# Four-layer graph network: reloads of a split matrix in small transfers, a ring of four row buffers, and one row block of layer 3 cast inside layer 2

## The chip, the cores and the metric

The kernel runs on one core of a Trainium2 chip. A core has TensorE (PE; its weight loads are listed as PEld), VectorE (DVE), ScalarE (ACT), GpSimd (POOL), SyncE (SP) and DMA queues. SP, ScalarE and GpSimd issue the transfers. The metric is the device time in microseconds (us); lower is better.

## The reference

Four layers are applied to `x` (4096 rows of 256) with one dense 0/1 adjacency `adj` (4096 x 4096). Each layer ends in `x = layernorm(x + layer(x))`. Layers 0 and 1 (an attention over the graph and a convolution) are not touched. Layers 2 and 3 are, cut to what matters:

```python
# layer 2: two steps; R is adj + identity, each row divided by its sum
for n in range(2):
    A = top_p_attention(Xa)        # softmax of q @ k.T, cut to the largest terms
                                   # that hold 0.9 of a row, renormalized
    Xf = R @ Xf                    # "diffusion"
    Xa = A @ Xa                    # "attention"
    Z = Z + Xf @ U1[n].T + Xa @ U2[n].T
x = layernorm(x + layernorm(x + Z) * ln_g + ln_b)

# layer 3
agg = adj @ x / max(deg, 1)
x = layernorm(x + relu(concat([x, agg]) @ W + b))
```

## The kernel before

**Tiles.** The 4096 rows are 32 row blocks of 128 (`NB = 32`, `P = 128`). `X` holds the attention's right-hand side for all blocks. `XD` holds the right-hand side of the products with the adjacency, 32 blocks of 128 x 512 (a 256-wide value split into two parts of reduced precision); a block is 256 KB. The adjacency lies in DRAM twice: as fp32 (`adjs`) and as bytes (`nad`). An `adj_piece` is the part of one row block that belongs to four column blocks (256 KB); there are three buffers for it. `es[0]`, `es[1]` and `es[2]` each hold one row block of attention scores (128 x 4096, fp32). `kT` holds the keys.

**Step 0 and step 1 of layer 2.** Each step begins with `keys`, `spreads` and the scores of row blocks 0 and 1. Then a loop of `project(step, b)` multiplies two row blocks by two weight matrices into a PSUM tile of two banks (`ps_logit`, two of them). In step 1 SP loads what is already summed for the pair into `xb` (line 1490), ScalarE copies one half of the product to `X` (line 1491) and the other half to a tile called `part` or `dif` in turn (line 1493), GpSimd adds it to `xb` (line 1494) and issues the store back to `xd` (line 1495). There are two buffers of `xb` and one each of `part` and `dif`.

Then a hand-ordered loop (`tc.manual_schedule`) goes over the row blocks. For each block `b` it has eight stages `s`. In a stage TensorE transposes four column blocks of the scores (`turn`, line 1350), ScalarE copies them (line 1352), TensorE multiplies them with `X` (`gather`, line 1359), and beside it TensorE works on diffusion products (`adj_product`, line 180) two or three row blocks ahead. VectorE finds the cut of the next row block meanwhile (`nucleus`, among others lines 1147, 1151, 1201). `scores` (line 993) and its exponentials (line 995) run two row blocks ahead.

**The reloads.** Towards the end of a step no diffusion product is left that reads the old `XD`, and `XD` is loaded with the next right-hand side (`reload`, line 1211, on SP), four blocks at a time: seven reloads of 1 MB at the places in the tuple `freed`, as (row block counted from the last diffusion's, stage). The time that becomes free beside the last row blocks goes to products of the next stage (`early`, with `times`, line 1554): in step 0 the first three row blocks of step 1's diffusion, in step 1 the first five row blocks of layer 3. `early` asks for each piece two pieces ahead (`piece`, line 1545, on SP). SP issues its transfers in order.

**The end of step 1.** Behind the last row block's scores stands a flag (line 1751) that says whether an exact method has to be run (`mend`, line 1217); with these inputs it is not. After it comes a second hand-ordered stretch:

- `load_bytes` fetches the byte adjacency of layer 3's first eight row blocks into `es[2]` and `es[0]` (`nas`, line 1844), 4 MB in all with two transfers issued earlier.
- The attention of row block 31 is gathered in eight steps `g`. `ahead3` multiplies finished rows by layer 3's weight and stores the result to `xtd` and `xo`, for row blocks 29 and 30.
- `closing(31)` runs the two layernorms of the last block on GpSimd and VectorE.
- `cast3` turns the bytes of layer 3's row block 5 into fp32r in `kT`, as four quarters `a[0]` to `a[3]` (line 1856).
- Then nine pieces of `early` are left, a reload of `XD` blocks 28 to 30 (768 KB), two small loads `lasts` into `q`, `product(0)` to `product(3)` with the quarters of block 5 (line 1805), five more pieces of group 7, the rows of block 31 (`turned`, `weighted`, `ahead3` into `XD[31]`), six last matmuls (line 1836), and the load of the next 4 MB of bytes into `X` (`rows`).

**Layer 3.** `ready(b)` casts the bytes of a row block into eight-block pieces, by VectorE (line 1854) and ScalarE (line 1856) in turn; `products(b)` does its 32 matmuls (line 1887); `close(b)` adds bias and weights, applies relu and layernorm and stores. Row blocks 0 to 5 come finished from layer 2. The loop starts so:

```python
            ready(6)
            ready(7)
            rest = [2, 5, 0, 1, 3, 4]
            for b in range(6, NB):
                ps = products(b)
                if b + 2 < NB:
                    ready(b + 2)
```

Of the kernel before, what the change touches and what calls it, by code (L numbers as in the profile page):

```python
# [9 lines left out]
F32 = mybir.dt.float32  # L10
I32 = mybir.dt.int32
F32R = mybir.dt.float32r
# [11 lines left out]
P = 128  # L24
# [31 lines left out]
class Net:  # L56
# [757 lines left out]
    def layer2(self):  # L814
        nc, tc, NB, D, X, N = self.nc, self.tc, self.NB, self.D, self.X, self.N
        A = 64
        HALF = N // 2
        with ExitStack() as ctx:
# [388 lines left out]
            def reload(src, a, b):  # L1207

                for k in range(a, b, 4):
                    to = min(k + 4, b)  # L1210
                    nc.sync.dma_start(XD[:, k:to].bitcast(F32), src[k:to].rearrange("b p s d -> p b s d"))
# [236 lines left out]
            def weighted(xT, pz):  # L1448


                for c in range(2):
                    nc.tensor.matmul(pz, xT[:, c, :], wt[:, c].rearrange("p k m -> p (k m)"),  # L1452
                                     start=(c == 0), stop=(c == 1))
                return pz

            def bank():
                return psum.tile([P, 512], F32, name="ps_tp")

            def project(step, b):


                two = slice(b, b + 2)
                rows = lambda t: t.rearrange("b p d -> p b d")
                pl = psum.tile([P, 2, 512], F32, name="ps_logit", bufs=2)
                if step == 0 and b < 16:
                    pt = bank()
                    for q in range(2):
                        for c in range(2):
                            nc.tensor.transpose(pt[:, (2 * q + c) * P:(2 * q + c + 1) * P],
                                                X[:, b + q, c * P:(c + 1) * P], self.ident)  # L1470
                    xT = work.tile([P, 512], F32, name="aT", bufs=2)
                    nc.scalar.copy(xT, pt)
                    xT = xT.rearrange("p (q c m) -> p q c m", q=2, c=2)
                else:
                    xT = held(step, b, 2)
                for q in range(2):
                    for c in range(2):
                        nc.tensor.matmul(pl[:, q, :], xT[:, q, c, :], wt[:, c].rearrange("p k m -> p (k m)"),
                                         start=(c == 0), stop=(c == 1))
                xb = work.tile([P, 2, D], F32, name="xb", bufs=2)  # L1480
                if step == 0:
                    nc.scalar.copy(XD[:, two, 0, :], pl[:, :, :D])
                    nc.scalar.copy(xb, pl[:, :, D:])
                    nc.vector.tensor_sub(XD[:, two, 1, :], pl[:, :, :D], XD[:, two, 0, :].bitcast(F32))
                    nc.scalar.dma_start(rows(pd[two]), xb)
                    xs = work.tile([P, 2, D], F32, name="part", bufs=1)
                    nc.gpsimd.tensor_add(xs, X[:, two, :], affine.unsqueeze(1).to_broadcast([P, 2, D]))
                    nc.gpsimd.dma_start(rows(xd[two, :, 1, :]), xs)
                else:
                    nc.sync.dma_start(xb, rows(xd[two, :, 0, :]))  # L1490
                    nc.scalar.copy(X[:, two, :], pl[:, :, :D])
                    xs = work.tile([P, 2, D], F32, name=("part", "dif")[b // 2 % 2], bufs=1)
                    nc.scalar.copy(xs, pl[:, :, D:])
                    nc.gpsimd.tensor_add(xb, xb, xs)
                    nc.gpsimd.dma_start(rows(xd[two, :, 0, :]), xb)
# [82 lines left out]
            for step in range(2):  # L1578
# [33 lines left out]
                if step == 0:  # L1612
                    xb = base(step, 0)
# [5 lines left out]
                if step == 0:  # L1619
# [3 lines left out]
                dd = 2 + step  # L1623
                rows_of = (xfd, xtd)[step]
                banks, made = {}, []
                freed = ((-1, 4), (-1, 5), (-1, 6), (-1, 7), (0, 0), (0, 2), (0, 4)) if step == 0 else \
                    ((0, 4), (-1, 5), (-1, 6), (-1, 7), (0, 0), (0, 2), (1, 1))
                freed = {at: g for g, at in enumerate(freed)}
                if step == 0:
                    todo = [(k, g) for g in range(7) for k in range(3)]  # L1630
                else:
# [5 lines left out]
                with tc.manual_schedule(engines=five):  # L1637
                    for b in range(NB - 1):
# [14 lines left out]
                        for s in range(8):  # L1653
# [28 lines left out]
                            for _ in range(pieces[s]):  # L1682
                                next(beside)
                            if (b + dd - NB, s) in freed:
                                g = freed[b + dd - NB, s]
                                reload(rows_of, 4 * g, 4 * g + 4)
                            gather(pa, aTs.pop(0), s)
                            if s == 3 and step == 1 and b - 2 in done:
                                put = ahead3(b - 2, done.pop(b - 2), pz, queue=nc.gpsimd)
# [87 lines left out]
                with tc.manual_schedule(engines=five):  # L1777
# [8 lines left out]
                    for g in range(8):  # L1786
                        if g < 7:
                            aTs.append(turn(es[b % 3], g + 1))
                        if g in (0, 6):
                            put = ahead3(b - 2 + g // 6, h, weighted(xT, bank()))  # L1790
                        gather(pa, aTs.pop(0), g)
                        if g in (0, 3):
                            next(close)
                        if g in (1, 7):
                            whole(put)
                        if g == 5:
                            h = whole(close)
                            xT = turned(h[:, 0], bank())
# [9 lines left out]
                    next(close)  # L1808
                    next(close)
                    self.cast3(nas, 5, a, nc.scalar)  # L1810
                    for _ in range(4):
                        next(beside)
                    next(close)
                    whole(beside)
                    reload(xtd, NB - 4, NB - 1)
                    lasts = []
                    for k in range(2):
                        two = work.tile([P, 2, P], F32R, name="q", bufs=2)
                        nc.sync.dma_start(two.bitcast(F32), self.adjs[2 * k:2 * k + 2, :, NB - 1, :].rearrange("b p i -> p b i"))
                        lasts += [two[:, 0], two[:, 1]]  # L1820
                    rows = [X[:, 8 * i:8 * i + 8, :].rearrange("p b d -> p (b d)").bitcast(U8)
                            .rearrange("p (k i) -> p k i", k=8) for i in range(4)]
                    product(0)
                    for k in range(5):
                        t = piece(1, k, 7)
                        times(banks[k], t, 7, ks=range(3))
                    lasts.append(t[:, 3])
                    h = whole(close)
                    product(1)
                    xT = turned(h[:, 0], bank())  # L1830
                    product(2)
                    pz = weighted(xT, bank())
                    product(3)
                    whole(ahead3(b, h, pz, True))
                    for t, to in zip(lasts + [a[3][:, 7]], [banks[k] for k in range(5)] + [ps]):
                        nc.tensor.matmul(to, t, XD[:, b].rearrange("p s d -> p (s d)"), start=False, stop=True)
                    self.load_bytes(rows, 1, 0)
                self.ahead3 = nas, rows
                self.early3 = [banks[k] for k in range(5)] + [ps]

    def load_bytes(self, nas, it, g):
# [17 lines left out]
    def layer3(self):  # L1859
        nc, tc, NB, D = self.nc, self.tc, self.NB, self.D  # L1860
        G = 8
        with self.ctx3 as ctx:
# [6 lines left out]
            out = self.rows(self.out)  # L1869
            psum, ps1 = self.psum2, self.ps2  # L1870
            nas = self.ahead3
            pieces = {}

            def ready(b):
                it = b * P // self.IT
# [26 lines left out]
                self.layernorm(work, y, h)  # L1902
                nc.scalar.dma_start(out[:, b, :], y[:, 0])

            ready(6)
            ready(7)
            rest = [2, 5, 0, 1, 3, 4]
            for b in range(6, NB):
# [61 lines left out]
```

## Time and profile before

| | |
|---|---|
| time, three runs | 4001.58, 4007.29, 4010.75 us; median 4007.29 |
| the profiled execution | 4011.93 us, span 4010.2 us, mean granted TensorE clock 0.991 |
| busy over the span | TensorE 97%, VectorE 75%, ScalarE 68%, GpSimd 28% |
| step 0 of layer 2, last row block and what follows | about 2604 to 2662 us |
| step 1, projections after the scores | about 2737 to 2797 us |
| step 1, from the flag to layer 3 | about 3735 to 3807 us |
| layer 3 | 3807 us to the end |

A span is the time from the first to the last instruction of the profiled execution. Lines such as L1554 are lines of the kernel before. A wait is put down to the work that ended last ahead of it. Busy times of TensorE come from a model of the pipelined matmul: one of 512 columns is listed with 394 ns, but 32 in a row take 7.47 us, 233 ns each.

### The profile page before, as it was taken

To read this page: it belongs to the slowest core of one execution; us is meant where nothing else is said; L and a number is where in the kernel's file an instruction comes from. 1 tells how busy PE (TensorE), PEld (TensorE's weight loads), DVE (VectorE), ACT (ScalarE), POOL (GpSimd) and SP (SyncE) were. 2 spreads that over 40 slices of the span, in tenths; PEclk is the share of its full clock that TensorE was granted. 3 is DMA by queue.
4 is the path that set the end of the run, shared out by engine and by line. 5 is a ranking of instruction groups with operands and counts; after the bars stand their busy time and mean duration, and the time that the engine had idled before them with its cause. 6 is when DMAs were issued, how large, how long until landed. Compare 5 with 4: busy or idle time off the path is not lost. (4 is left out here: it accounts for less than half of the span.)

```text
span 4010.2 us, 68765 instructions
## 1 busy us (share of the span) xinstructions
PE 3906.8 (97%) x25081; PEld 3377.3 (84%) x25081; DVE 2990.2 (75%) x6647; ACT 2742.6 (68%) x5119; POOL 1136.7 (28%) x1394
## 2 busy tenths in 40 slices
PE   8899998999999899999999999999999999999899
PEld 7899998999999788678888888865888888888687
DVE  7742228999999444567878788837999999999365
ACT  5532228999999322468888888825888888888132
POOL 1321111111344022411111111114555555555211
PEclk9999999999999999999999999999999999999999
DMA  4765557335222498533333333463333333335541
GB/s 130 228 204 176 176 168 224 90 108 136 69 78 70 170 359 324 154 119 96 100 97 101 95 102 92 137 203 105 108 107 104 108 118 99 107 120 184 186 158 49
DMA packets 317403, 557.36 MB, mean 139 GB/s; under 512 B 72646, under 2 KB 139734, under 8 KB 312950
## 3 DMA queue, kind: packets, MB, share of 16 engines
q1 hardware_dynamic: 242368, 396.99, 31.4%
q0 software_dynamic: 32224, 98.75, 7.5%
q10 hardware_dynamic: 42454, 57.04, 4.3%
q8 instruction: 203, 3.33, 0.3%
q14 instruction: 154, 1.26, 0.1%
HBM read 386.71 MB, written 165.94 MB: 138 GB/s over the span
## 5 line engine op out<-in xcount | busy, mean ns | idle before, releaser
L1359 PE MATMUL ps_a<-X,aT 128*128 128x256 f32 x4096 | 970.4, 379 | 1.3 <-ACT h L1500 1.1
L1359 PEld LDWEIGHTS ps_a<-X,aT 128*128 128x128 f32 x4096 | 774.1, 190 | 127.2 <-issue 3.3
L328 PE MATMUL acc<-gm,gt 128*128 128x198 bf16 x8192 | 702.5, 248 | 14.2 <-DVEq L366 5.6
L328 PEld LDWEIGHTS <-gt 128*128 128x128 fp8e4 x8192 | 700.4, 97 | 16.2 <-issue 11.3
L273 ACT ACTIVATE sg<-lpb,nlc 128x1024 fp8e4<-128x1024 f32 x632 | 664.0, 1135 | 48.5 <-DVE gt L275 33.8
L550 PE MATMUL pz<-src,ar 128*128 128x264 f32 x4096 | 513.5, 288 | 20.6 <-DVE ar L540 18.6
L550 PEld LDWEIGHTS pz<-src,ar 128*128 128x128 f32 x4096 | 510.3, 191 | 23.7 <-DVE ar L540 21.3
L180 PE MATMUL ps_r<-XD,adj_piece 128*128 128x512 f32 x1888 | 528.4, 414 | 1.0 <-DMA adj_piece<-adjs 1.0
L1086 ACT ACTIVATE ja<-e,nc 128x2048 uint8<-128x2048 f32 x240 | 480.9, 2004 | 2.0
L1352 ACT COPY aT<-ps_tp 128x512 f32<-128x512 f32 x512 | 296.4, 579 | 216.7 <-PE ps_tp L1350 214.5
L180 PEld LDWEIGHTS ps_r<-XD,adj_piece 128*128 128x128 f32 x1888 | 332.9, 189 | 70.2 <-issue 12.9
L1151 DVE MAX8 cand<-v 128x8 f32<-128x256 f32 x1024 | 347.1, 411 | 4.4
L1201 DVE SCALAR_TENSOR_TENSOR e<-e,edge 128x512 f32<-128x512 f32 x512 | 347.9, 751 | 2.1
L543 ACT ACTIVATE nb<-ar 128x512 uint8<-128x512 f32 x256 | 147.5, 623 | 268.4 <-DVE ar L540 265.2
L1350 PE MATMUL ps_tp<-ident,e 128*128 128x128 f32 x2048 | 307.7, 273 | 0.0
L1147 DVE SCALAR_TENSOR_TENSOR v<-e,hi 128x2048 f32<-128x2048 f32 x128 | 299.8, 2342 | 2.4
L1350 PEld LDWEIGHTS ps_tp<-ident,e 128*128 128x128 f32 x2048 | 256.5, 141 | 51.4 <-issue 0.5
L267 DVE TENSOR_SCALAR sg<-lpb,nlc 128x1024 fp8e4<-128x1024 f32 x384 | 285.2, 778 | 6.6 <-SPq L366 4.4
L995 ACT ACTIVATE e<-ps_logit 128x1024 f32<-128x1024 f32 x256 | 260.2, 1027 | 26.6 <-PE ps_logit L993 26.4
L993 PE MATMUL ps_logit<-kT,q 128*128 128x512 f32 x1024 | 274.1, 409 | 4.0 <-ACT e L995 1.7
L540 DVE CAST ar<-a 128x1024 fp32r<-128x1024 f32 x128 | 88.9, 695 | 248.1 <-PE pz L550 242.4
L802 PE MATMUL ps_adj<-XD,adj_piece 128*128 128x512 f32 x1024 | 244.9, 398 | 1.2 <-POOL ln_var L88 1.2
(396 smaller groups left out, 5577.5 us busy)
## 6 DMA issues: line engine op xcount, KB each, us to landing
adj_piece<-adjs SPq DMA_DIRECT2D x552, 256.0 KB, 2.9
a<-in_adjt_dram SPq DMA_DIRECT2D x256, 256.0 KB, 3.0
adjs<-adj_piece SPq DMA_DIRECT2D x96, 512.0 KB, 3.4
na<-nad SPq DMA_DIRECT2D x64, 512.0 KB, 4.5
lpb<-lpd POOLq DMA_DIRECT2D x32, 512.0 KB, 4.2
nad<-nb POOLq DMA_DIRECT2D x128, 128.0 KB, 2.8
na<-nad ACTq DMA_DIRECT2D x16, 1024.0 KB, 5.6
gmd<-gb POOLq DMA_DIRECT2D x64, 198.0 KB, 3.9
```

Source lines behind the costliest of these rows:

```text
L180: nc.tensor.matmul(ps, a[:, k, :], rhs(jc).rearrange("p s d -> p (s d)"), start=(jc == 0), stop=(jc == self.NB - 1))
L267: nc.vector.tensor_scalar(sg[:, k, :], lpb, nlc[:, 4 * g + k, h:h + 1], 2.0 ** -5, op0=ALU.is_ge, op1=ALU.mult, saturate=False)
L273: nc.scalar.activation(sg[:, k, :], lpb, AF.Sign, scale=-1.0, bias=nlc[:, 4 * g + k, h:h + 1], saturate=False)
L328: nc.tensor.matmul(acc[:, q, :6 * C1], gt[:, k, q * P:(q + 1) * P], gm0[:, jc, :] if head0 else gm[:, jc, hh, :], start=(jc == 0 and q % 2 ...
L550: nc.tensor.matmul(pz[q][:, t, :W], ar[:, q, k, :], src[:, jc, t, s], start=(jc == 0 and s == 0), stop=(jc == NB - 1 and s == 1))
L1086: nc.scalar.activation(ja, e[:, s * HALF:(s + 1) * HALF], f, bias=nc1, accum_out=fs[:, i + s:i + s + 1])
L1147: nc.vector.scalar_tensor_tensor(v, ec, hi, ec, op0=ALU.is_lt, op1=ALU.mult, accum_out=sb[:, s:s + 1])
L1151: nc.vector.max(cand[:, 8 * j:8 * j + 8], v[:, k * 256:(k + 1) * 256])
L1201: nc.vector.scalar_tensor_tensor(ec, ec, edge[:, j:j + 1], ec, op0=ALU.is_ge, op1=ALU.mult)
L1350: nc.tensor.transpose(pt[:, k * P:(k + 1) * P], e[:, jc * P:(jc + 1) * P], self.ident)
L1352: nc.scalar.copy(aT, pt)
L1359: nc.tensor.matmul(pa[:, :D], aT[:, k * P:(k + 1) * P], X[:, jc, :], start=(jc == 0), stop=(jc == NB - 1))
```

## The change

1. **Reloads in small transfers.** `freed` now gives each place a range of blocks. In step 0 the 28 blocks come in ten reloads of 4, 3, 3, 4, 4, 3, 2, 2, 2 and 1 blocks instead of seven of 4; in step 1 in twelve of 3, 3, 3, 3, 2, 2, 2, 2, 2, 2, 2 and 2. Blocks 28 to 30 at the end of step 1 come one at a time: two within the last gather and one after it.
2. **A ring of four in step 1.** Of the sixteen projections of step 1, numbers 2 to 12 take `xb` and the second half's copy from `es[2]`: four places of 512 columns for each. The others keep the tiles they had.
3. **The end of step 1.** Three pieces of `early` move into the last gather (at `g` 3, 5 and 7), as do the two `lasts` loads (at `g` 3); three instead of four pieces stand ahead of the last `next(close)`.
4. **Row block 6 of layer 3 is cast in layer 2.** After `product(i)` has used the quarter `a[i]` of block 5, ScalarE casts the same quarter of block 6 over it; the last one follows the six last matmuls. Layer 3 takes these as `pieces[6]` and its `ready(6)` goes.

```diff
@@ project @@
-                xb = work.tile([P, 2, D], F32, name="xb", bufs=2)
+                nth = (b - 16) % NB // 2
+                ring = [es[2][:, i + nth % 4 * 512:i + nth % 4 * 512 + 512].rearrange("p (q d) -> p q d", d=D)
+                        for i in (0, 2048)] if step and 2 <= nth <= 12 else ()
+                xb = ring[0] if ring else work.tile([P, 2, D], F32, name="xb", bufs=2)
...
-                    xs = work.tile([P, 2, D], F32, name=("part", "dif")[b // 2 % 2], bufs=1)
+                    xs = ring[1] if ring else work.tile([P, 2, D], F32, name=("part", "dif")[b // 2 % 2], bufs=1)
@@ ahead of the loop over row blocks @@
-                freed = ((-1, 4), (-1, 5), (-1, 6), (-1, 7), (0, 0), (0, 2), (0, 4)) if step == 0 else \
-                    ((0, 4), (-1, 5), (-1, 6), (-1, 7), (0, 0), (0, 2), (1, 1))
-                freed = {at: g for g, at in enumerate(freed)}
+                if step == 0:
+                    freed = {(-1, 4): (0, 4), (-1, 5): (4, 7), (-1, 6): (7, 10), (-1, 7): (10, 14), (0, 0): (14, 18),
+                             (0, 1): (18, 21), (0, 2): (21, 23), (0, 3): (23, 25), (0, 4): (25, 27), (0, 5): (27, 28)}
+                else:
+                    freed = {(-1, 5): (4, 7), (-1, 6): (7, 10), (-1, 7): (10, 13), (0, 0): (13, 16), (0, 1): (16, 18),
+                             (0, 2): (18, 20), (0, 3): (20, 22), (0, 4): (22, 24), (0, 5): (0, 2), (0, 6): (2, 4),
+                             (1, 1): (24, 26), (1, 2): (26, 28)}
...
-                                g = freed[b + dd - NB, s]
-                                reload(rows_of, 4 * g, 4 * g + 4)
+                                reload(rows_of, *freed[b + dd - NB, s])
@@ the last gather @@
+                        if g in (3, 5, 7):
+                            next(beside)
                         gather(pa, aTs.pop(0), g)
+                        if g in (2, 4):
+                            k = NB - 5 + g // 2
+                            reload(xtd, k, k + 1)
+                        if g == 3:
+                            lasts = []
+                            for k in range(2):
+                                two = work.tile([P, 2, P], F32R, name="q", bufs=2)
+                                nc.sync.dma_start(two.bitcast(F32),
+                                                  self.adjs[2 * k:2 * k + 2, :, NB - 1, :].rearrange("b p i -> p b i"))
+                                lasts += [two[:, 0], two[:, 1]]
@@ after it @@
                     self.cast3(nas, 5, a, nc.scalar)
-                    for _ in range(4):
+                    for _ in range(3):
                         next(beside)
                     next(close)
+                    reload(xtd, NB - 2, NB - 1)
                     whole(beside)
-                    reload(xtd, NB - 4, NB - 1)
-                    lasts = []
-                    ...
                     product(0)
                     ...
                     lasts.append(t[:, 3])
+                    self.cast3(nas[:1], 6, a[:1], nc.scalar)
                     h = whole(close)
                     product(1)
                     xT = turned(h[:, 0], bank())
+                    self.cast3(nas[1:2], 6, a[1:2], nc.scalar)
                     product(2)
                     pz = weighted(xT, bank())
                     product(3)
+                    self.cast3(nas[2:3], 6, a[2:3], nc.scalar)
                     whole(ahead3(b, h, pz, True))
                     for t, to in zip(lasts + [a[3][:, 7]], [banks[k] for k in range(5)] + [ps]):
                         nc.tensor.matmul(to, t, XD[:, b].rearrange("p s d -> p (s d)"), start=False, stop=True)
+                    self.cast3(nas[3:], 6, a[3:], nc.scalar)
                     self.load_bytes(rows, 1, 0)
-                self.ahead3 = nas, rows
+                self.ahead3, self.sixth = (nas, rows), a
@@ layer3 @@
-            pieces = {}
+            pieces = {6: self.sixth}
...
-            ready(6)
             ready(7)
```

More of the change, by code (lines that the diff above doesn't have):

```diff
@@ L1810, in layer2 @@
                     self.cast3(nas, 5, a, nc.scalar)
-                    for _ in range(4):
+                    for _ in range(3):
                         next(beside)
                     next(close)
+                    reload(xtd, NB - 2, NB - 1)
                     whole(beside)
-                    reload(xtd, NB - 4, NB - 1)
-                    lasts = []
[L1817 to L1820, printed above, removed]
                     rows = [X[:, 8 * i:8 * i + 8, :].rearrange("p b d -> p (b d)").bitcast(U8)
```

## The prediction

> **What bounds the kernel now.** I read the page from the top, then TensorE's waits and timeline in the three stretches where its busy line dips inside layer 2.
>
> ```profile
> PE 3906.8 (97%) x25081; PEld 3377.3 (84%) x25081; DVE 2990.2 (75%) x6647; ACT 2742.6 (68%) x5119; POOL 1136.7 (28%) x1394
> PE   8899998999999899999999999999999999999899
> ```
>
> TensorE is busy for 97% of the span, so an edit pays only where TensorE stands idle or runs at a lower clock: about 103 us in all. The change adds no matmul and takes none away. TensorE's waits at the end of step 0 (2604 to 2662 us), at the start of step 1 (2735 to 2797) and at the end of step 1 (3735 to 3812), as us in total, times, longest:
>
> ```profile
> PE ps_logit L1554 <- DMA adj_piece<-adjs: 6.8, 4, 2.5
> ...
> PE ps_logit L1478 <- ACT part L1493: 1.6, 2, 1.0
> PE ps_logit L993 <- ACT dif L1493: 1.1, 1, 1.1
> PE ps_logit L993 <- ACT part L1493: 1.1, 1, 1.1
> ...
> PE ps_logit L1554 <- DMA adj_piece<-adjs: 6.4, 8, 2.0
> PE ps_tp L1443 <- PEq L1217: 3.8, 1, 3.8
> PE ps_tp L1887 <- DVE adj_piece L1854: 3.3, 1, 3.3
> PE ps_logit L1554 <- POOLq L1217: 1.9, 1, 1.9
> ```
>
> Adjacency pieces come late at both ends, the copies into `part`/`dif` come late at the start of step 1, and layer 3's first cast comes late at the handover. The 3.8 is the branch after the flag and the 1.9 a POOL operation; the change touches neither. Why the pieces are late is in SP's own waits, step 1's start first, then its end:
>
> ```profile
> SPq L1490 <- DMA xd<-xb: 60.3, 14, 10.6
> ...
> SPq L1545 <- DMA xo<-h: 5.3, 1, 5.3
> ```
>
> The first: an `xb` load waits until the store from the same buffer has landed. The second: one piece load of the last stretch stands behind the store of the last row block. What the gaps cost is more than their idle time, as the stretches 3772:3784, 3784:3796 and 3804:3812 show (busy us by engine, granted clock, DMA share, GB/s):
>
> ```profile
> 3772.00:3784.00 12.00, 9.65 (x37) 6.33 (x36) 1.22 (x4) 3.94 (x5) 6.30 (x9) 1.00 0.65 197
> 3784.00:3796.00 12.00, 8.06 (x26) 5.61 (x25) 0.00 (x0) 0.00 (x0) 0.00 (x0) 0.86 0.66 224
> 3804.00:3812.00 8.00, 4.72 (x15) 3.80 (x16) 3.62 (x6) 3.89 (x4) 0.00 (x0) 0.79 0.48 159
> ```
>
> **What the Trainium skill says.** "TensorE: Matmul & The Clock Gate", Part 1, says that TensorE falls to half clock after an idle window and needs some us of work to come back. The trace agrees: clock 0.86 and 0.79 above, and gathers (L1359) of 631 ns after the gap at 2633 where the usual one takes 379. "DMA: Bandwidth & Descriptors", Bandwidth, advises batches of 1 MiB or more. Here a piece of 256 KB lands in 2.9 to 3.1 us and reloads of 1 MB in 7.7 to 8.0 (one measured in each step), but the question is who stands behind the big one. The same page, "Issuing engines are not separate DMA queues", says that all queues share the 16 engines; 414 GB/s at share 1.00 between 3796 and 3804 is this core's ceiling in the trace. "SBUF — State Buffer" says VectorE and GpSimd lock a shared port against each other; POOL's adds (L1494) of 1.25 to 4.35 us for one shape fit that, though part of the long ones is waiting for `xb`.
>
> **1. Handover to layer 3: -4.8.** Now the last matmul of layer 2 starts at 3803.54, VectorE's first cast waits until 3806.49 for the landing of `xo<-h` (4.73 us), and the products start at 3807.28: 3.3 idle. Their first 64 matmuls take 16.45 us, later ones 14.93: 1.5 more at low clock. After: block 6 is cast on ScalarE into `kT` as soon as each quarter of block 5 is used, four times 1.04 us (L1856). Queued behind them on ScalarE are the `xT` copy and the copies for `XD[31]`. The first cast falls under the fifteen `times` matmuls, the second under product(2) (1.86 us), the third under the projection and product(3); the fourth waits for the last matmul, and the 24 products before its quarter last 5.6. So they cost nothing; if that cover failed, 1 to 2 us. Block 7's casts still wait for `xo<-h`, under 7.5 us of block 6. Bounds 2 to 5.
>
> **2. The tail of step 1: -6.8.** From 3771.30 to 3795.13 TensorE does 59 matmuls (nine pieces, product(0), fifteen for group 7). At 7.47 us per 32 they need 13.8; they take 23.8, so 10.0 is lost. The new order puts three pieces (2.8 us) into the gather loop, where their loads are already in; the gather ends at 3774.1 and 47 matmuls remain (11.0). SP's queue, walked with 3.1 us a landing and three buffers: the fourth late piece comes 1.0 late, the sixth 0.7 (block 30's reload, 256 KB instead of 768 KB for three blocks, is ahead of it), the fourth of group 7 1.5. Lost 3.2. In the built queue no piece waits for the last block's store: that wait belongs to the reuse of a DMA semaphore, and the new numbering gives it to an older transfer. The closing chain of the last block (9.0 us from gather end to `h`) starts 2.8 later and is ready at 3783, used about 3790. The reload of block 29 holds SP until its store lands (about 3759); the piece behind it is used at 3774. Bounds 3 to 9.
>
> **3. Step 1's ring: -5.0.** One buffer now goes through load 3.0, add 1.3 to 1.7, semaphore and issue 1.0, store 2.7: 8.2 us, or 4.1 per pair with two buffers; a pair's matmuls need 3.45 (8 at 0.431, from 40 in 17.43). Fourteen pairs at that pace end at 2786.4, then eight transposes and eight score matmuls (2.8) bring the first gather to 2789.2 instead of 2794.68: 5.4. With four places the memory cycle is 2.1 per pair, POOL's add and issue 2.3, ScalarE's two copies 1.2: TensorE sets the pace. VectorE must have row block 0 ready: it waits 6.4 us for POOL's `inv` (L1182), which stands behind the adds; its inputs are there at 2778.5, so the first edges are done about 2781. POOL then waits up to 3 us for VectorE at `above`, which four places bridge. The ring lies in `es[2]`; its last store lands about 2783, before the scores of block 2 overwrite it at 2788. I take 5.0 for a first wait that stays. Bounds 2 to 5.4.
>
> **4. Step 0's reloads: -4.2.** Of four long gaps in pieces two follow 1 MB reloads in the last row block (1.71 and 2.19, 0.2 of small ones); after the second the matmuls run slow for 1.6. Together 5.7. A third of 2.46 follows the 1 MB reload of blocks 28 to 31, which stays. Half-size reloads take 1.3 us less at 390 GB/s (slices of this stretch), about the slack of a piece; I leave 0.5 in each of three stages. Bounds 0 to 5.7.
>
> **5. Step 1's reloads before the flag: -0.3.** One gap of 1.0 behind a 1 MB reload at 3669 may halve; blocks 26 and 27 now come one stage later, 3.6 to 4.5 us before use. Bounds -1 to +1.5. The ten additional transfers in both steps cost SP 0.4 us each to issue; its queue is mostly waiting there. VectorE and ScalarE lose four casts in layer 3, where they wait for TensorE: nothing.
>
> **Sum:** 4.8 + 6.8 + 5.0 + 4.2 + 0.3 = 21.1. The profiled execution took 4011.9 (span 4010.2, 1.7 around it), so it would take 3990.8; it lies 4.6 above the median of 4007.3, so the forecast is **3986**. A difference of 0.2%, 8 us, is about what this measurement can tell from none.
>
> **The rivals.**
> - *Forecast*, 0.56: all five within their bounds, 3980 to 3993.
> - *Bytes, not order*, 0.20: the ends are held by the volume, so steps 2, 4 and 5 give only 1 together and handover and ring 8.8: 3997.5. For it: 263 GB/s between 2604 and 2636 already. Against it: the slices there reach 390, and stage 4 of that block runs three pieces without a wait.
> - *No gap left*, 0.13: 10.0 + 4.8 + 5.4 + 5.7 + 1.0 = 26.9: 3980, down to 3976. Against it: the piece loads still have three buffers and 3 us of latency.
> - *A wait at every small reload*, 0.05, the slower side: SP issues in order, and a reload that waits for an older store or for its semaphore holds the pieces behind it. About fourteen stages now have one; at 2.2 us each (today's gap) this is 31, less 8.8: 4029. It decides from 0.6 us per stage, where gain is used up, and the result is slower beyond 1.2. Against it: in the built queue the waits it adds are on transfers several loads back.
> - *Not what it says*, 0.06: the built order or a bank keeps the handover or the ring as it was, 3991 to 4000.
>
> The range 3977 to 3999 leaves out the slower rival, part of the second and little of the third. Faster 0.86, within 0.2% 0.09, slower 0.05.
>
> **What would show it.** Right: layer 3's products follow the last layer 2 matmul within 0.5 us, their first 64 take about 15; no wait on `part`/`dif` in step 1's projections and the first gather 5 us earlier; SP without the 5.3 on `xo<-h`; the 1.7 and 2.2 gaps under 1. Wrong: piece waits of 1 us in most stages, an idle TensorE behind ScalarE's casts, or a clock under 0.9 after 3772.

## The result, and the profile after

The kernel after takes **3988.26 us** (median of five, 3981.79 to 3996.39) against 4007.29 of the kernel before (five, 4001.58 to 4012.31). The ratio is 0.9953, 95% interval 0.9941 to 0.9965. The profiled execution of after took 3996.39 us, span 3994.6, granted clock 0.991: 8.1 above its own median, where that of before lay 4.6 above.

The page: busy us by engine, then TensorE's busy tenths over 40 slices.

```profile
PE 3901.5 (98%) x25081; PEld 3375.7 (85%) x25081; DVE 2997.9 (75%) x6645; ACT 2747.6 (69%) x5121; POOL 1160.1 (29%) x1394
PE   8899998999999899999999999999999999999899
```

TensorE has the same 25081 matmuls, and the line of tenths is unchanged: the whole result lies under its resolution, in gaps of 0.5 to 5 us. They show in TensorE's waits at the end of step 0 (2604 to 2662 us), the start of step 1 (2735 to 2797) and its end (3735 to 3812):

```profile
PE ps_logit L1557 <- DMA adj_piece<-adjs: 4.2, 3, 2.6
...
PE ps_tp L1350 <- DVE e L1201: 1.9, 2, 1.4
...
PE ps_logit L1557 <- DMA adj_piece<-adjs: 4.5, 5, 1.5
PE ps_tp L1443 <- PEq L1217: 3.8, 1, 3.8
```

Pieces late: 6.8 became 4.2 in step 0 and 6.4 became 4.5 in step 1. The copies into `part` and `dif` hold TensorE no more, but a wait for VectorE's edges has come. No wait for a layer 3 cast is left; the branch after the flag is as it was. (Lines of the kernel after: L1493 is the load of `xb`, L1496 the copy of the second half, L1497 GpSimd's add, L1548 `piece`, L1557 `times`, L1823 `product`, L1852 the last matmuls, L1861 `load_bytes`, L1904 layer 3's products.) SP's own waits, first the start of step 1, then its end:

```profile
SPq L1493 <- DMA xd<-e: 31.2, 7, 10.6
...
SPq L1548 <- PE ps_logit L1557: 19.2, 9, 6.6
SPq L1861 <- DVE adj_piece L1871: 14.9, 1, 14.9
SPq L1211 <- DMA xtd<-part: 7.4, 1, 7.4
```

The loads of the ring still make SP wait, but TensorE waits for nothing behind them. The 5.3 on `xo<-h` is gone; most of what the pieces wait for is a buffer that TensorE frees, as it was before (33.4 there).

The tail in TensorE's timeline (start, us, line, operation, and in brackets the idle time ahead of it), from the last gather to `product(1)`:

```profile
3766.91 3.16 PE L1557 MATMUL ps_logit<-XD,adj_piece 128*128 128x512 f32 x12
3770.91 1.20 PE L1557 MATMUL ps_logit<-XD,adj_piece 128*128 128x512 f32 x4 [0.84 <-DMA adj_piece<-adjs]
3772.85 2.41 PE L1557 MATMUL ps_logit<-XD,adj_piece 128*128 128x512 f32 x8 [0.74 <-DMA adj_piece<-adjs]
...
3780.75 0.96 PE L1557 MATMUL ps_logit<-XD,adj_piece 128*128 128x512 f32 x3 [1.48 <-DMA adj_piece<-adjs]
3782.32 1.46 PE L1557 MATMUL ps_logit<-XD,adj_piece 128*128 128x512 f32 x3 [0.61 <-DMA adj_piece<-adjs]
3783.58 3.12 PE L1823 MATMUL ps_a<-XD,kT 128*128 128x512 f32 x8
3786.54 0.38 PE L1443 MATMUL ps_tp<-ident,h 128*128 128x128 f32 x2
```

And the handover:

```profile
3792.86 0.39 PE L1852 MATMUL ps_logit<-XD,adj_piece 128*128 128x512 f32 x1
3793.09 0.39 PE L1852 MATMUL ps_a<-XD,kT 128*128 128x512 f32 x1
3793.32 7.43 PE L1904 MATMUL ps_tp<-XD,kT 128*128 128x512 f32 x32
3800.59 7.63 PE L1904 MATMUL ps_tp<-XD,adj_piece 128*128 128x512 f32 x32
```

Layer 3 follows without a gap and at full pace: `kT`, cast in layer 2, feeds its first 32 matmuls.

To place the gain I cut each profile at points of TensorE's timeline: **A** from the first gather of step 0's last row block to step 1's main run of projections, **B** from there to the first gather of step 1, **C** on to the first gather behind step 1's flag, **D** on to the matmuls with the last rows, **E** on to layer 3's third row block, **F** the rest.

| | start | A | B | C | D | E | F | span |
|---|---|---|---|---|---|---|---|---|
| before | 2608.25 | 129.67 | 56.76 | 958.13 | 49.57 | 21.20 | 186.62 | 4010.2 |
| after | 2609.45 | 125.31 | 53.69 | 957.19 | 46.30 | 16.12 | 186.54 | 3994.6 |
| after, second profile | 2609.44 | 125.74 | 53.68 | 957.93 | 46.10 | 16.12 | 186.59 | 3995.6 |

Gains 4.4, 3.1, 0.9, 3.3, 5.1 and 0.1, less 1.2 lost ahead of the change: 15.6. The untouched first part took 2600.1 to 2609.5 us in the profiles of this study, so spans are no measure for a part; the stretches are. They vary too, but with one exception, C, the two profiles that have the old form of a part lie outside all that have the new one (kernels whose own edit bears on the stretch left out): A 129.7 and 131.7 against 123.2 to 125.7, B 56.8 and 56.5 against 53.6 to 55.2, D 49.6 and 49.0 against 44.1 to 47.7, E 21.2 and 21.3 against 16.1.

### The profile page after: what moved, and what is told of

Its sections match the earlier page's. It is cut to its first block, busy times and chain, and to the rows that moved or that the text cites. A ratio compares the mean times of both kernels' runs of the same rounds, so it can differ in the third digit from the quotient of the medians.

```text
span 3994.6 us, 68784 instructions
## 1 busy us (share of the span) xinstructions
PE 3901.5 (98%) x25081; PEld 3375.7 (85%) x25081; DVE 2997.9 (75%) x6645; ACT 2747.6 (69%) x5121; POOL 1160.1 (29%) x1394
## 5 line engine op out<-in xcount | busy, mean ns | idle before, releaser
L1350 PEld LDWEIGHTS ps_tp<-ident,e 128*128 128x128 f32 x2048 | 256.8, 142 | 53.6 <-DVE e L1201 3.0
```

What stands on the lines that cost most here:

```text
L1350: nc.tensor.transpose(pt[:, k * P:(k + 1) * P], e[:, jc * P:(jc + 1) * P], self.ident)
```

## The experiments

Each kernel is the kernel after with one edit, where nothing else is said. Times are medians; the kernel before, timed beside each, had medians of 4005.0 to 4007.6. The number behind a median is its ratio to that, with its 95% interval.

### Each part undone

**No ring**: every projection uses `xb`, `part` and `dif` again.

```diff
-                        for i in (0, 2048)] if step and 2 <= nth <= 12 else ()
+                        for i in (0, 2048)] if False else ()
```

> The changed kernel without the ring of four: step 1's projections load, scale and add through the two-deep xb tile and the single part and dif tiles again. Theory (the ring's gain is bounded by VectorE's first edges): the stretch from the first projection of the last 13 pairs to step 1's first gather, 53.7 us in the changed kernel, goes back to 56.8, TensorE's waits there are again on ScalarE's and GpSimd's copies, and the median rises by 2.5 to 3.5 us. Rival (the ring itself cost something, through GpSimd's adds that now run against VectorE's small operations): VectorE's first edge comes no earlier with the ring than without, and the median rises by under 1.5 us. If the prediction's own figure held, it would rise by 5.

B 56.46 instead of 53.69; median 3993.76 (ratio 0.9957, 0.9940 to 0.9974). TensorE's waits in this stretch:

```profile
PE ps_logit L993 <- ACT dif L1496: 1.8, 1, 1.8
PE ps_logit L1478 <- ACT part L1496: 1.6, 2, 1.0
```

The old waits are back and the wait for edges is gone: 2.8 us, the theory's size and about half of the 5 predicted. One bound has been exchanged for another, and a part of the rival is there too: VectorE starts its first edge 48.5 us after the projections' start with the ring and without it. In three of eight profiles with the ring the clock drops after the wait for edges and B is 55.2; there the ring gives 1.3. The timings don't decide the size: the median is 5.5 above that of after, the ratio 0.0004, or 1.6 us, with an interval of 7 us on either side.

**No sixth block**: the four casts out of layer 2, `ready(6)` back in layer 3.

```diff
-                    self.cast3(nas[:1], 6, a[:1], nc.scalar)    # and the three others
-            pieces = {6: self.sixth}
+            pieces = {}
+            ready(6)
             ready(7)
```

> The changed kernel with layer 3's seventh block cast in layer 3 again, after layer 2's last product. Theory: TensorE waits some 3.3 us for the first casts and then runs its first matmuls at a lower clock, so the stretch from the product with the last rows to the third layer 3 block's first product grows by 4.5 to 5.5 us, and the median rises by about 5. Rival (the casts' loads or VectorE's share of them set the time anyway, or the casts in the tail had slowed the tail on ScalarE): under 2.5 us.

E 21.32 instead of 16.12, +5.2; D 46.42, unchanged; median 3996.97 (0.9965, 0.9951 to 0.9979). TensorE's timeline:

```profile
3788.50 0.40 PE L1849 MATMUL ps_a<-XD,kT 128*128 128x512 f32 x1
3792.12 16.71 PE L1900 MATMUL ps_tp<-XD,adj_piece 128*128 128x512 f32 x64 [3.22 <-DVE adj_piece L1867]
```

3.2 us idle and 64 matmuls in 16.7 us. The ratio is 0.0012 above that of after, 4.8 us. The rival falls: D is the same with and without the casts, so on ScalarE in the tail they cost nothing that shows.

**Old reloads**: groups of four blocks at the old places in both steps.

```diff
+                freed = ((-1, 4), (-1, 5), (-1, 6), (-1, 7), (0, 0), (0, 2), (0, 4)) if step == 0 else \
+                    ((0, 4), (-1, 5), (-1, 6), (-1, 7), (0, 0), (0, 2), (1, 1))
+                freed = {at: (4 * g, 4 * g + 4) for g, at in enumerate(freed)}
```

> The changed kernel with both steps' reloads in groups of four row blocks again (seven of 1 MB, at their old places); the tail and its single-block reloads stay as changed. Theory: step 0's last three piece waits come back (1.71 and 2.19 us with a slow clock behind them), so the start of step 1's projections is 4 to 4.5 us later, and the stretch ahead of step 1's flag is about 1.3 us longer; the median rises by 5 to 6 us. Rival (the stalls there come from the bytes, which are the same, and not from their order): under 2 us.

A 131.72, 6.4 more than after, and 2 more than before, which has the same reloads: one gap was 3.5 us here and 2.2 there. C 958.82 lies within the spread of this stretch (956.6 to 959.1). The median, 3990.26 (0.9951, 0.9935 to 0.9968), 2 above that of after and not the 5 to 6 expected, hides it in the spread of runs. Waits at the end of step 0:

```profile
PE ps_logit L1557 <- DMA adj_piece<-adjs: 8.7, 4, 3.5
```

The same 7 MB in much the same stages: 8.7 us of waiting in seven transfers, 4.2 in ten. The bytes are not what held the stretch. The pieces show it themselves: in the 45 us from just ahead of the last row block on, those of 256 KB landed 5.9 us (median) after their issue here, 5.7 in before, and 3.2 to 3.8 in nine profiles with the new reloads. Smaller transfers and more places for them came together; which of the two does it is not separated.

**Old tail**: `reload(NB - 4, NB - 1)` in one transfer and the `lasts` loads behind all the pieces, none between the gathers; the casts of block 6 stay.

```diff
-                        if g in (3, 5, 7):
-                            next(beside)
-                        if g in (2, 4):
-                            k = NB - 5 + g // 2
-                            reload(xtd, k, k + 1)
...
-                    for _ in range(3):
+                    for _ in range(4):
                         next(beside)
                     next(close)
-                    reload(xtd, NB - 2, NB - 1)
                     whole(beside)
+                    reload(xtd, NB - 4, NB - 1)
```

> The changed kernel with the order of step 1's tail as it was (reloads of three blocks in one transfer and the two small loads of the last rows after all the pieces but the last group, no pieces between the gathers), but with the seventh block's casts kept in layer 2. Theory (the order took away SyncE's wait and the pieces' queue): TensorE loses about 10 us between the last gather and the product with the last rows instead of 5.7, and the median rises by 2.5 to 4.5 us. Rival (SyncE's 5.3 us wait for the last block's store in the kernel before came from how DMA completions were numbered over the queues, which any edit shifts, and not from the order): that wait is gone here too, TensorE loses 6 us or less, and the median rises by under 1.5 us.

D 48.96, against 49.57 before and 46.1 as the mean of nine profiles with the new tail (44.1 to 47.7); median 3994.54 (0.9965, 0.9951 to 0.9980). TensorE's waits for pieces in the tail, then SP's waits there:

```profile
PE ps_logit L1557 <- DMA adj_piece<-adjs: 5.8, 7, 2.7
```

```profile
SPq L1548 <- PE ps_logit L1557: 7.0, 8, 1.2
SPq L1548 <- DMA adj_piece<-adjs: 4.5, 2, 4.0
```

SP's wait on `xo<-h` is gone although the order is the old one, as the rival says. That the numbering of the transfers decides which of them a load waits for fits this, but no run changes the numbering alone. A wait of 4.0 for an earlier piece has taken its place, and TensorE waits 5.8 for pieces where before had 6.3 and the nine profiles 3.0 to 4.0; this the rival does not explain. So the name of the wait cost little: 0.6 us lie between this D and that of before, less than the spread from profile to profile. The order cost 2.8 on the mean.

### Why the ring gave 3 and not 5

**No adds**: GpSimd's additions left out in the last eight pairs.

```diff
-                    nc.gpsimd.tensor_add(xb, xb, xs)
+                    if nth < 8:
+                        nc.gpsimd.tensor_add(xb, xb, xs)
```

> The changed kernel without GpSimd's additions in the last eight pairs of step 1's projections (their sums are left out of the base, so the output lacks those terms); copies, loads and stores stay. Theory (the shared port): VectorE's three long small operations (1.70, 1.60 and 1.92 us on 40, 1 and 8 columns) fall to about 0.25 each, the first edge comes 4 to 7 us earlier, and TensorE's wait of 1.9 us for edges is gone, so the first gather is 2 us earlier in its stretch. Rival (those operations wait for an operand from another engine, whichever it is): they stay above 1 us and the wait stays.

B 51.33, 2.4 less than after and 5.4 less than before; the wait for edges is gone (one run, 3982.96). VectorE and GpSimd in after, then VectorE here:

```profile
2776.14 1.70 DVE L1177 SCALAR_TENSOR_TENSOR tmp<-top,cuts,kept 128x40 f32<-128x40 f32 x1
2779.25 1.60 DVE L1188 TENSOR_TENSOR nxt<-nxt,hi 128x1 f32<-128x1 f32 x1
2781.27 1.92 DVE L1197 TENSOR_SCALAR edge<-edge,cuts 128x8 f32<-128x8 f32 x1
2783.23 6.78 DVE L1201 SCALAR_TENSOR_TENSOR e<-e,edge 128x512 f32<-128x512 f32 x8
```

```profile
2776.49 1.28 POOL L1497 TENSOR_TENSOR e<-e 128x512 f32<-128x512 f32 x1
2779.54 1.29 POOL L1497 TENSOR_TENSOR e<-e 128x512 f32<-128x512 f32 x1
2781.87 1.28 POOL L1497 TENSOR_TENSOR xb<-xb,dif 128x512 f32<-128x512 f32 x1
```

```profile
2765.77 0.26 DVE L1177 SCALAR_TENSOR_TENSOR tmp<-top,cuts,kept 128x40 f32<-128x40 f32 x1
2767.45 0.16 DVE L1188 TENSOR_TENSOR nxt<-nxt,hi 128x1 f32<-128x1 f32 x1
2768.03 0.22 DVE L1197 TENSOR_SCALAR edge<-edge,cuts 128x8 f32<-128x8 f32 x1
2768.28 5.39 DVE L1201 SCALAR_TENSOR_TENSOR e<-e,edge 128x512 f32<-128x512 f32 x8
```

Each of the three stretched operations begins just ahead of an add and ends within 0.1 us of it. The Trainium skill, "SBUF — State Buffer", Terms, says that VectorE and GpSimd take a shared port pair for a whole instruction and the loser blocks; the trace agrees: an operation on one column takes 1.60 us beside an add of 1.29, and 0.16 without. Without the adds VectorE starts its first edge 44.2 us after the projections' start instead of 48.5. Up to the first of the three operations it is equally far in both (41.7 and 41.4 us), and together the three are 4.6 us shorter, so they account for all of it.

**Estimate later**: block 1's estimate written behind block 0's edges in the program.

```diff
                 if step == 1:
                     whole(scores(1, queries(1)))
-                    guess = drained(guessed(step, 1))
...
+                    if b == 14 and step == 1:
+                        guess = drained(guessed(step, 1))
```

> The changed kernel with row block 1's estimate in step 1 (two scans of 4096 columns on VectorE, 5.3 and 4.5 us, and its small ScalarE operations) put into the program after row block 0's edges instead of before its selection. Nothing else is moved. Theory (what is left between step 1's projections and its first gather is VectorE's queue: block 1's scans run ahead of block 0's edges): VectorE's first edge, 48.5 us after the first of the last 13 projections in the changed kernel, comes at about 39 to 42 us; TensorE's two waits for edges (0.5 and 1.4 us) go; the stretch from the projections' start to the first gather falls from 53.7 to about 51.5, and the ring is then worth the 5 us that the prediction gave it. Rival 1 (GpSimd's adds on the shared port stretch VectorE's work wherever it stands): the edge comes under 4 us earlier and a wait of a microsecond stays. Rival 2 (the time is only moved): the stretch from the first gather to the flag, 938.9, grows by 2 us or more because block 1's selection is late.

B 56.67, 3 us longer; median 3990.80 (0.9961, 0.9950 to 0.9973). No expectation was met: the first edge comes 51.1 us after the projections' start, later than in after. This part is not ordered by hand, and the program's scheduler still put the scans ahead of the edges on VectorE; on ScalarE block 1's operations then stood waiting for VectorE's scan with the copies behind them. VectorE, then TensorE's waits:

```profile
2756.28 4.47 DVE L1080 SCALAR_TENSOR_TENSOR v<-e,c 128x4096 bf16<-128x4096 f32 x1
2762.00 4.47 DVE L1009 SCALAR_TENSOR_TENSOR v<-e,c 128x4096 bf16<-128x4096 f32 x1
2777.71 2.48 DVE L1201 SCALAR_TENSOR_TENSOR e<-e,edge 128x512 f32<-128x512 f32 x1
```

```profile
PE ps_logit L1478 <- ACT e L1496: 2.7, 1, 2.7
PE ps_tp L1350 <- DVE e L1201: 0.7, 1, 0.7
```

**Scores later**: block 1's scores and estimate at the eleventh projection, so that the scans do stand behind the edges.

```diff
-                    if b == 16 and step == 0:
+                    if b == (16, 22)[step]:
                         whole(scores(1, queries(1)))
                         guess = drained(guessed(step, 1))
```

> The changed kernel with row block 1's whole first pass in step 1 (its scores, 32 matmuls and four exponentials, and its estimate with the two scans on VectorE) taken from ahead of the projections to the eleventh pair of them, as step 0 does it; here the two scans stand behind block 0's edges on VectorE. The same instructions run, in another order. Theory (block 1's scans ahead of block 0's edges are what TensorE waits for, with GpSimd's adds stretching them): the edges are done before the last projections are, TensorE's waits of 0.5 and 1.4 us and the slower clock behind them go, and the stretch from the end of the estimate's spreads to the first gather gets 2 to 3.5 us shorter. Rival (the time is moved on: block 1's selection becomes late, and TensorE waits for its edges in the first row): the stretch from the first gather to the flag, 938.9, gets as much longer.

A and B together (32 score matmuls move from one to the other) take 181.51 against 179.00; median 3993.21 (0.9957, 0.9942 to 0.9973); C 956.95, so nothing was moved into the rows. VectorE has its first edge free of adds at 2763.5, 21 us before the last projection ends, as wanted. But the scheduler drew the first transpose of those edges ahead of the last 40 projection matmuls, and TensorE took them up only behind it:

```profile
2764.34 0.47 PE L1350 MATMUL ps_tp<-ident,e 128*128 128x128 f32 x1 [3.63 <-DVE e L1201]
2764.60 20.07 PE L1478 MATMUL ps_logit<-wt,X 128*128 128x512 f32 x40
```

So neither theory nor rival: the old wait went and a new one of 3.6 came. That block 1's scans cost the ring its last 2 us is thus not shown; that GpSimd's adds do, is.

### What is left in step 0 and in the tail

**Block 31 alone**: blocks 28 to 30 before the flag, one block after it.

```diff
-... (0, 4): (25, 27), (0, 5): (27, 28)}
+... (0, 4): (25, 27), (0, 5): (27, 28), (0, 6): (28, 30), (0, 7): (30, 31)}
...
-                    reload(rows_of, NB - 4, NB)
+                    reload(rows_of, NB - 1, NB)
```

> The changed kernel with step 0's last 1 MB reload cut: row blocks 28 to 30 are brought back in the last row block's stages 6 and 7, and only block 31 (256 KB) after the flag. Theory (the 2.65 us gap and the slow clock behind it come from the pieces queued behind 1 MB): the gap falls under 1 us, and the stretch from the last row block's first gather to the start of step 1's projections falls from about 125 us by 2.5 to 4. Rival (TensorE waits there for the flag's way through SyncE and the branch, which the reload only covers): the gap stays within 0.7 us of 2.65, or another wait of the same size takes its place.

Median 3988.13 (0.9957, 0.9942 to 0.9972). Waits at the end of step 0, where after had one of 2.6 for a piece and 0.3 for the flag:

```profile
PE ps_r L1557 <- PEq L1217: 1.8, 1, 1.8
PE ps_logit L1557 <- DMA adj_piece<-adjs: 1.2, 3, 0.5
PE ps_r L1557 <- DMA adj_piece<-adjs: 1.0, 1, 1.0
```

The longest gap, 2.65 and then 0.30 in after, became 0.99 and 1.77: the same sum, with the branch in the place of the reload. A is 123.55, within the 123.2 to 125.7 of the kernels whose step 0 is that of after. The rival is right: the 1 MB covered the flag's way.

**Mixed**: two matmuls of layer 3's second product behind each of the first four of the last five pieces.

```diff
                         times(banks[k], t, 7, ks=range(3))
+                        product(1, slice(2 * k, 2 * k + 2))
...
-                    product(1)
```

> The changed kernel with the second product of layer 3's sixth block (8 matmuls, 2.0 us) no longer after the five pieces of the last group but spread over them, two matmuls behind each of the first four; the loads are in the same order. Theory (in the tail the pieces come at the pace of their transfers, so independent matmuls between them are free): the stretch from the last gather to the product with the last rows, 24.7 us in the changed kernel, falls by 1.5 to 2.5 us. Rival (each piece's load waits for a buffer that TensorE frees, so that a busier TensorE delays the loads by the same time): under 0.7 us.

D 43.93, 2.4 less than after; median 3988.89 (0.9955, 0.9939 to 0.9972), with B at 55.21 in this profile. A single D of 43.9 says little, as the nine profiles without this edit reach down to 44.1; but the two kernels below that have it too show 42.7 and 42.8, and the waits for pieces in the tail fall to 1.7 to 2.2 us from 3.0 to 4.0. Independent matmuls between late pieces are free here.

**All three**: scores later, mixed, and thinner pieces: the first four pieces of the last group without their fourth block, which no matmul reads from them.

```diff
-                nc.sync.dma_start(a.bitcast(F32), self.adjs[b, :, 4 * g:4 * g + 4, :])
+                nc.sync.dma_start(a[:, :n].bitcast(F32), self.adjs[b, :, 4 * g:4 * g + n, :])
...
-                        t = piece(1, k, 7)
+                        t = piece(1, k, 7, n=3 + (k == 4))
```

> Three edits to the changed kernel at once: block 1's first pass in step 1 later (as in scores_late), layer 3's second product spread over the five pieces of the tail (as in mix), and the first four of those pieces loaded without their fourth block of 64 KB, which nothing reads. Theory (the two remaining waits are independent): 2 to 3.5 us at the first gather, 2.2 for the product and up to 1 for the 256 KB less (at the 215 GB/s that the tail moved, 256 KB take 1.2 us): the span stands 4 to 6.5 us under the changed kernel's, the ratio to the kernel before at about 0.994 where the changed kernel's was 0.9953. Rival (the close of the last row block, which the last product waits for, is the next limit in the tail): the tail gains no more than mix alone, and the whole 4 us or less.

D 42.73, but A and B 181.56 as with the scores later: 3987.78 (0.9954, 0.9940 to 0.9968). The expectation held in the tail and missed at the first gather, and so in the whole, where 0.994 was expected.

**After, again**, beside it:

> The changed kernel once more, beside the two others on the same chip. Expected: 3986 to 3990 us at the median, a ratio of 0.9945 to 0.996 to the kernel before; its stretches as in its first profile within half a microsecond, but for the places where the clock drops after a wait (up to 1.5 us at the first scores of row block 2, and up to 1.3 in the tail).

3988.02 (0.9947, 0.9933 to 0.9960); its stretches are in the table above.

**The tail's two edits alone**:

> The two edits of the tail alone: layer 3's second product spread over the five last pieces, and the first four of those pieces loaded as 192 KB instead of 256. The step 1 projections stay as in the changed kernel. Theory: from the last gather to the product with the last rows about 21 us as in the run with all three edits (24.7 and 24.5 in the changed kernel's two profiles), and 53.7 us (55.2 where the clock drops) from the projections to the first gather: the median is 3 to 4 us under the changed kernel's, 3983 to 3986, and the ratio to the kernel before about 0.994. Rival (what the tail gains is within the spread of the runs): the profile shows the shorter tail and the median still lies within 1.5 us of the changed kernel's 3988.

D 42.83, 3.5 less than after, A 123.19, B 53.64; median **3982.21** (3979.51 to 3986.92), the lowest here among kernels that compute everything, but the kernel before beside it had its lowest median too, 4005.02; ratio 0.9946 (0.9933 to 0.9960). Waits in the tail, then TensorE's timeline where the first late piece begins and where `product(1)` is done:

```profile
PE ps_logit L1557 <- DMA adj_piece<-adjs: 2.2, 3, 0.8
```

```profile
3759.74 3.16 PE L1557 MATMUL ps_logit<-XD,adj_piece 128*128 128x512 f32 x12
...
3775.91 0.38 PE L1443 MATMUL ps_tp<-ident,h 128*128 128x128 f32 x2
```

The same 55 matmuls (47 and the 8 of `product(1)`) take 16.17 us here and 19.63 in after (3766.91 to 3786.54, shown with the result). The granted clock behind them, in the third column from the end, here and then in after:

```profile
3775.00:3783.00 8.00, 7.89 (x32) 5.81 (x33) 0.96 (x3) 3.15 (x6) 0.00 (x0) 1.00 1.01 420
```

```profile
3784.00:3792.00 8.00, 8.00 (x30) 5.82 (x29) 0.96 (x3) 3.04 (x5) 0.00 (x0) 0.88 0.96 396
```

The profile shows the 3.5 us. The timings do not: the ratio, 0.9946, is that of the second timing of after, 0.9947, so that this kernel is faster than after is not settled.

## Why the prediction was right

The forecast was 3986, the time 3988.3. Four of the five mechanisms are there; the fifth moved a wait and gained nothing that shows. That the number came so close is in part luck. The profiles differ by 15.6 where 21.1 was predicted, the medians by 19.0: the profiled execution of after lies 8.1 above its median and that of before 4.6, and this difference of 3.5 hides most of the 5.5 that are missing. By steps, predicted and measured in the profiles:

- **1. Handover, 4.8: 5.1.** 3.3 of idle and 1.5 at low clock were both right; the run without the sixth block gives 5.2 back.
- **2. Tail, 6.8: 3.3.** The failing term is "Lost 3.2". It compared unlike things: 10.0 was elapsed time over need, 3.2 a sum of idle times. The waits came nearly as walked (1.0, 0.7, 1.5 predicted; 0.84, 0.74, 1.48 measured, and an unforeseen 0.61). But the 47 matmuls from 3766.91 to 3783.58 took 16.67 us for the 10.97 they need, so 5.7 were lost: 3.7 as listed waits, 1.1 beside them (0.23 to 0.36 at each), and 0.9 within two groups of matmuls where no wait is listed. Then product(1) took 3.12 us instead of 2.0, at a granted clock of 0.59. In before, 6.3 of listed waits had stood for 10.0 of loss; that ratio on 3.2 would have given 5.1.
- **3. Ring, 5.0: 3.1.** "TensorE sets the pace" was right: the last 88 projection matmuls ran through in 38.03 us. The failing term is "the first edges are done about 2781". GpSimd's `inv` did come early, 43.5 us after the projections' start instead of 47.1, but its adds, no longer waiting for buffers, now met VectorE's small operations; the first edge was done 6 us later than the prediction has it. Without half of the adds B is 51.3, which is what the prediction's sum gives for it (2789.2 less 2737.9).
- **4. Step 0, 4.2: 4.4.** Two gaps of 0.82 and 0.70 where 0.5 in each of three was assumed. The prediction's 2.9 to 3.1 us for the landing of a piece do not hold here: it was 5.7 in this stretch of before. That the third gap belongs to the 1 MB reload was wrong in its cause and harmless in the sum: it is the flag's way.
- **5. Before the flag, 0.3: not resolved.** The gap of 1.0 at 3670 is gone in all twelve profiles with the new places and there in both with the old ones. But a gap of 0.3 to 1.2 us (0.47 in after) now stands some 36 us later, so the wait was moved and not halved. C was 957.2 and 957.9 against 958.1, and 956.6 to 959.1 in the others.

Of the rivals, "Bytes, not order" fell with the old reloads: same bytes, 6.4 us more in A. "A wait at every small reload" did not come: 4.2 us of piece waits in step 0, fewer than before. "No gap left" was right at the handover and wrong in the tail, where pieces in three buffers stay 0.6 to 1.8 us late in the two profiles of after. Two slips in the prediction change nothing: its rivals count 8.8 for handover and ring where its steps have 4.8 and 5.0, and the trace lists 4.43 us for VectorE's wait ahead of the first cast, not 4.73.

## What to carry to other kernels

Compare like with like in a stretch: elapsed time minus need on both sides, not elapsed time on one and listed waits on the other. When a wait in an in-order queue has a striking name, undo the order and see whether the name comes back before paying for it; here the name changed and the loss stayed. Judge a single profile by the spread of the same stretch in others: after the same wait the clock fell in some and not in others. When buffers are added, ask what the freed engine will now run beside: GpSimd's adds met VectorE's small operations, and these took 4.6 us longer.

## What the runs showed of the hardware

- Three VectorE operations on 1 to 40 columns that met a GpSimd add ended within 0.1 us of it, whatever their size: 1.60 us for one column, 0.16 in the run without the adds.
- After the 1.4 us wait for edges the next eight score matmuls took 2.1 us in some profiles and 3.4 to 3.7 in others (three of eight), with the same instructions around them. The granted clock over them was 1.00 in the five and 0.51 to 0.57 in the three. The Trainium skill, "TensorE: Matmul & The Clock Gate", Part 1, describes a clock that falls after idling; that it falls after 1.4 us only sometimes is what these runs add.
- Loads of 256 KB issued on SP among reloads of 1 MB took 5.7 and 5.9 us to land, and 3.2 to 3.8 where the same bytes came in smaller reloads at more places.
- The start of a load can wait for a transfer of another engine's queue that has nothing to do with it: in before the profile puts 5.3 us of SP's waiting down to `xo<-h`, a store that ScalarE issues. In the kernel with the old tail there is no such wait; what gave it to this store in before stays open.
